# Where the butterflies of gate's and up's weights are written: a tile of their own, or the loaded tile's places

## The chip, the cores and the metric

The kernel runs on one core of a Trainium2 chip. The metric is the device time of one execution in microseconds, the median of several runs. The engines are called PE (TensorE, the matmuls), DVE (VectorE), ACT (ScalarE), POOL (GpSimd) and SP (SyncE, which here issues nearly all DMAs).

## The reference

All numbers are float32. x has 8 sequences of 512 tokens with 512 features.

```python
xn = _layernorm(x, axis=-1)
s = _L0_attn_ref(xn, ...)          # q, k, v; phi = elu + 1; kv_sum = cumsum(phi_k * v); (phi_q * kv_sum) @ Wo.T + bo
g = _silu(_L0_ffn_ref(xn, ...))
x = x + s * g
...
x = fwht(x * SU_ug) / SCALE        # _L0_ffn_ref, fwht: Walsh-Hadamard transform over the last dimension
x_up = x @ W_up.T * (Wscale_ug[:INTER] * SCALE)
x_gate = x @ W_gate.T * (Wscale_ug[INTER:] * SCALE)
x = jax.nn.silu(x_gate) * x_up
x = fwht(x * SU_dp) / SCALE
x = x @ W_down.T * (Wscale_dp * SCALE)
```

W_up and W_gate are 2048 x 512, W_down is 512 x 2048. The transform of 512 features is linear, so it can be applied to the weights instead of the tokens: the kernel does that once, on the chip ("folding").

## The kernel before, in words

**Products.** Every matrix product is made with seven products of half-size blocks in place of eight (a Strassen-like scheme). The seven places have names, P1, P2, P7, P3, P4, P5, P6, in this order of storage. A weight tile `w` is 128 x (2, 7, 128): j, one of two halves of the rows contracted; s, one of the seven places; 128 columns. Four places (P1, P2, P7, P4) are loaded, the others are sums that DVE makes in `encode_weights` (lines 312 to 315, four additions of 128x256). A `group` (line 449) multiplies one such tile with all tokens of two sequences; PE works in three PSUM banks (px, py, pz), ACT copies px out (L470), and DVE adds such a copy to py or pz (L476).

**Order of the work.** The 8 sequences are taken in pairs p = 0 to 3. Each pair: attention (k, v, q for two groups of heads), then four units u of the feed-forward part (gate, up, each in two tiles f = u and f = u + 4), each unit's hidden block `ho`, and after units 1 and 3 a product with the down weights (L536) into tiles `dn`, one of which is `d_0`, `d_1` for the two sequences; they are stored to DRAM by `put_by` (L752) as d_d. In pair 0 the weights are raw. For u = 0, 1, 2 they are loaded by `first_w`, into tiles from the pool `wpool` (4 buffers). For u = 3 `weights_ahead` (L1061) does it while unit 1's down product is on PE, into tiles of the pool `t8`. After folding, the tiles of f >= 4 are combined with those of f - 4 (`inner_w`, L397 to 422: additions of 128x896 at L412, stores at L404), and from then on all weights come from DRAM in their final form. So all 16 foldings (8 of gate, 8 of up) fall in pair 0.

**One folding** is `folded_w` (L926 to 962), as three steps that an agenda spreads over the program: the raw load (`raw_w`, four DMAs at L354, the weights of four 128x128 blocks per j), `butterflies` (L934: a Hadamard step over two index bits, four DVE operations of 128x512 at L937 to L940), `fold` (L943: the other seven bits, as two products with the constant matrix `had`, L946, each of four passes of 512 columns, since float32 is done in four passes; ACT scales the result back into `w` at L952, four copies of 128x256), and `encode` (L955).

**Pools.** `t8` has 6 buffers of 8 KB in each partition (one has 2 x 7 x 128 or 2 x 2 x 512 floats). It holds `r` of the butterflies (L935), the gates `g` and ups `u`, the down outputs `dn`, the tiles `wd` of the down weights, `w` of unit 3, and more. A new tile takes a place that an earlier one used, and its first writer waits until the last reader of the earlier one is done; a store to DRAM is such a reader. Which instructions stand where on each engine is set by the scheduler of the framework from priorities, data and buffers; where `later` and `pace` (L77, L80) are used, small pieces of work are put behind given instructions. SP issues its DMAs in one queue in order, so a DMA that waits holds back those behind it.

**The down weights** are folded as well, in four columns of blocks (`butterflies_down`, L979 and L984, `fold_down`, L998 and L1004), on a tile `rd` of its own; the tiles `wd` get their sums through `down_w` (the additions show as L93 and L99 because `pace` and `catch_up` call them). POOL encodes some `ho` and co (L304 to 307) and multiplies gate with up (L802).

Of the kernel before, what the change touches and what calls it, by code (L numbers as in the profile page):

```python
# [8 lines left out]
F32 = mybir.dt.float32  # L9
AF = mybir.ActivationFunctionType  # L10
ALU = mybir.AluOpType
# [10 lines left out]
def kernel(  # L22
# [27 lines left out]
    nc = tc.nc  # L50
    P = 128
# [16 lines left out]
    t8 = ctx.enter_context(tc.tile_pool(name="t8", bufs=6))  # L68
# [5 lines left out]
    @contextmanager  # L74
    def background(behind=150):

        at = tc.cur_priority  # L77
        tc.cur_priority = at + behind
        yield
        tc.cur_priority = at  # L80
# [23 lines left out]
    at = 0  # L104
# [12 lines left out]
    had = const.tile([P, P], F32, tag="had", name="had")  # L117
# [192 lines left out]
    def encode_weights(eng, w):  # L310
        w = w.rearrange("p j s e -> p s j e") if len(w.shape) == 4 else w
        eng.tensor_tensor(w[:, P5], w[:, P7], w[:, P4], ALU.add)
        eng.tensor_tensor(w[:, P6], w[:, P5], w[:, P1], ALU.subtract)
        eng.tensor_tensor(w[:, P3], w[:, P2], w[:, P6], ALU.subtract)
        eng.tensor_tensor(w[:, P7], w[:, P1], w[:, P7], ALU.subtract)
# [30 lines left out]
    def raw_w(name, src, n0, dn, step, c0, dc, w=None):  # L346

        w = new_w(name) if w is None else w
        for a in range(2):
            tiles = src[:, c0 + a * dc : c0 + a * dc + P].rearrange("(n p) e -> p n e", p=P)  # L350
            for b in range(2):
                n = n0 + b * dn
                place = (P1, P2, P7, P4)[2 * a + b]
                nc.sync.dma_start(w[:, :, place, :], tiles[:, n : n + step + 1 : step])  # L354
        return w
# [41 lines left out]
    def inner_w(m, u, w0, w1):  # L397

        if u not in inner:
            inner[u] = dram.tile([P, 7, 2, 7, P], F32, tag=f"d_gu_{u}", name=f"d_gu_{u}")  # L400
        d = inner[u][:, :, ("gate", "up").index(m)]

        def store(c, t):
            nc.sync.dma_start(d[:, :, c, :], t)  # L404

        store(P1, w0[:, 0])
        store(P2, w0[:, 1])
        store(P4, w1[:, 1])
        t = xin.tile([P, 3, 7, P], F32, tag="x", name=f"s_{m}_{u}")

        def made(c, i, a, b, op):
            nc.vector.tensor_tensor(t[:, i], a, b, op)  # L412
            store(c, t[:, i])

        later(1.0, made, P5, 0, w1[:, 0], w1[:, 1], ALU.add, soon=True)
        later(1.0, made, P6, 1, t[:, 0], w0[:, 0], ALU.subtract, soon=True)
        later(1.0, made, P3, 2, w0[:, 1], t[:, 1], ALU.subtract, soon=True)

        def last():
            later(1.0, made, P7, 0, w0[:, 0], w1[:, 0], ALU.subtract, soon=True)  # L420

        later(0.0, at, 8, last, soon=True)
# [503 lines left out]
    def folded_w(name, src, f, room=None):  # L926

        w = raw_w(f"{name}_{f}", src, 0, 2, 1, f * P, NG * P, room)
        places = (slice(P1, P7 + 1, 2), slice(P2, P4 + 1, 3))
        rs = []  # L930

        def butterflies():
            t = t8.tile([P, 2, 2, 2, 2, P], F32, tag="t", name=f"r_{name}_{f}")
            r2, r = t[:, 0], t[:, 1]  # L934
            rs.append(r)  # L935
            a, b = (w[:, :, place, :] for place in places)
            nc.vector.tensor_tensor(r2[:, 0], a, b, ALU.add)  # L937
            nc.vector.tensor_tensor(r2[:, 1], a, b, ALU.subtract)
            nc.vector.tensor_tensor(r[:, :, 0], r2[:, :, 0], r2[:, :, 1], ALU.add)
            nc.vector.tensor_tensor(r[:, :, 1], r2[:, :, 0], r2[:, :, 1], ALU.subtract)  # L940

        def fold():
            for b in range(2):  # L943
                p = ps.tile([P, 2, 2, P], F32, tag="t", name=f"pw_{name}_{f}_{b}")
                tc.keep_in_program_order(
                    nc.tensor.matmul(  # L946
                        p.rearrange("p j a e -> p (j a e)"), had,
                        rs[0][:, b].rearrange("p j a e -> p (j a e)"), start=True, stop=True,
                    )
                )  # L950
                for j in range(2):
                    nc.scalar.activation(  # L952
                        w[:, j, places[b], :], p[:, j], AF.Copy, scale=su_ug[:, 2 * b + j : 2 * b + j + 1]
                    )
        def encode():  # L955
            encode_weights(nc.vector, w)
            folded[name, f] = w
            if f >= NU:
                with background():
                    inner_w(name, f - NU, folded[name, f - NU], w)  # L960

        return w, [(5, butterflies), (7, fold), (9, encode)]

    folded = {}
# [75 lines left out]
    def first_w(m, g):  # L1040


        if m == "gate":
            return folded_w(m, wgate_t, g)
        if m == "up":
            return folded_w(m, wup_t, g)
        name, eng = f"{m}_{g}", nc.gpsimd if m == "o" else nc.vector
        if m == "o":
            t = new_w(name)
            w = by_factor(t)  # L1050
            rows_w(w, wo_t, g, 2)
        else:
            t = w = raw_w(name, sources[m], 0, 2, 1, g * P, 2 * P)

        def encode():
            encode_weights(eng, w)
            keep_w(name, t)

        return w, [(5, encode)]

    def weights_ahead(u):  # L1061

        def begin(m, src, f):
            t = t8.tile([P, 2, 7, P], F32, tag="t", name=f"w_{m}_{f}")
            _, steps = folded_w(m, src, f, t)
            place = 10
            for _, step in steps:
                at(place, step)
                place += 7

        at_ = 2
        for m, src in (("gate", wgate_t), ("up", wup_t)):
            for f in (u, u + NU):
                at(at_, lambda m=m, src=src, f=f: begin(m, src, f))
                at_ += 12
# [65 lines left out]
    for i in range(7):  # L1141
        dst = had if i % 2 == 0 else had2
        s = src.rearrange("p (a t h) -> p a t h", t=2, h=1 << i)
# [18 lines left out]
    rs = rd[:, : 3 * NF * P].rearrange("p (i c e) -> p i c e", i=3, e=P)  # L1162
# [141 lines left out]
```

## Time and profile before

| | us |
|---|---|
| runs | 1551.83, 1550.75, 1551.32 |
| median | 1551.32 |
| profiled execution, span (its own time, first to last instruction) | 1552.4 |
| PE busy | 1523.8 |
| DVE busy | 1002.4 |
| ACT busy | 418.9 |
| POOL busy | 436.7 |

By stretches of the span (busy us of each engine, granted PE clock as a share of full speed):

| stretch | PE | DVE | ACT | POOL | clock |
|---|---|---|---|---|---|
| 0 to 70 (no folding yet) | 61.31 | 61.93 | 31.31 | 7.83 | 1.00 |
| 70 to 345 (the 16 foldings) | 264.18 | 213.63 | 98.30 | 71.38 | 0.99 |
| 345 to 1552.4 | 1198.26 | 726.81 | 289.25 | 357.47 | 1.00 |

A row of a timeline has the start in us, the duration in us, the engine, the line of the kernel, the operation, out<-in by the program's names, partitions x elements, the count of instructions run together (x4), and in brackets the idle time of the engine before it with what ended it. SPq means the queue of SP, where only issuing is shown. "f32" is the type. A share of a stretch in which PE is busy is an average: what matters is which wait ends last ahead of PE.

### The profile page before, as it was taken

To read this page: it belongs to the slowest core of one execution; us is meant where nothing else is said; L and a number is where in the kernel's file an instruction comes from. 1 tells how busy PE (TensorE), PEld (TensorE's weight loads), DVE (VectorE), ACT (ScalarE), POOL (GpSimd) and SP (SyncE) were. 2 spreads that over 40 slices of the span, in tenths; PEclk is the share of its full clock that TensorE was granted. 3 is DMA by queue.
4 is the path that set the end of the run, shared out by engine and by line. 5 is a ranking of instruction groups with operands and counts; after the bars stand their busy time and mean duration, and the time that the engine had idled before them with its cause. 6 is when DMAs were issued, how large, how long until landed. Compare 5 with 4: busy or idle time off the path is not lost.

```text
span 1552.4 us, 15693 instructions
## 1 busy us (share of the span) xinstructions
PE 1523.8 (98%) x5924; PEld 1121.3 (72%) x5924; DVE 1002.4 (65%) x1423; ACT 418.9 (27%) x664; POOL 436.7 (28%) x236
## 2 busy tenths in 40 slices
PE   7989999999999999999999999999999999999998
PEld 3436446746874588888884488888886478888887
DVE  7989787378867665516767674715675575533673
ACT  4452341141125411112114431111213431111211
POOL 1232233004320261205511144302621126210631
PEclk9999999999999999999999999999999999999999
DMA  8345877687985244354576344335574233535462
GB/s 276 98 141 176 258 250 240 214 276 261 267 283 162 90 154 160 95 166 164 166 265 235 93 143 149 114 119 186 175 245 155 87 112 102 191 100 174 164 258 81
DMA packets 197692, 273.31 MB, mean 176 GB/s; under 512 B 56816, under 2 KB 155120, under 8 KB 193392
## 3 DMA queue, kind: packets, MB, share of 16 engines
q1 hardware_dynamic: 197472, 272.27, 54.0%
q8 instruction: 47, 0.77, 0.2%
q14 instruction: 29, 0.24, 0.0%
q10 hardware_dynamic: 144, 0.03, 0.0%
HBM read 196.25 MB, written 76.02 MB: 175 GB/s over the span
## 4 chain that ended last, share of the span: by engine, by line
PE 90%; DVE 6%; DMA 1%; ACT 1%; issue 1%; SPq 0%; POOL 0%; POOLq 0%; DVEq 0%; ACTq 0%
PE px_gu L638 20%; PE px_dn L536 13%; PE pz_gu L638 10%; PE pz_dn L536 6%; PE py_gu L638 5%; PE px_k L460 4%; PE py_dn L536 4%; PE px_o L536 3%; PE px_v L460 3%; PE px_q L460 3%; PE px_up L460 2%; PE pz_o L536 2%; PE pz_k L460 2%; PE pz_v L460 2%; PE pz_q L460 2%; PE px_gate L460 1%
## 5 line engine op out<-in xcount | busy, mean ns | idle before, releaser
L638 PE MATMUL px_gu<-xo,w_gu 128*128 128x256 f32 x1456 | 347.7, 380 | 1.4 <-DVE sb_gu L648 1.4
L638 PEld LDWEIGHTS px_gu<-xo,w_gu 128*128 128x128 f32 x1456 | 275.7, 190 | 45.9 <-issue 5.0
L536 PE MATMUL px_dn<-w_down,ho 128*128 128x256 f32 x1024 | 228.7, 379 | 0.0
L536 PEld LDWEIGHTS px_dn<-w_down,ho 128*128 128x128 f32 x1024 | 194.6, 190 | 28.6 <-issue 2.4
L638 PE MATMUL pz_gu<-xo,w_gu 128*128 128x256 f32 x728 | 187.7, 380 | 1.1 <-DVE u L476 1.1
L838 POOL TENSOR_TENSOR u<-u,v 128x1024 f32<-128x1024 f32 x26 | 61.0, 2367 | 365.9 <-DVE u L676 347.4
L638 PEld LDWEIGHTS pz_gu<-xo,w_gu 128*128 128x128 f32 x728 | 137.5, 190 | 22.3 <-DVE u L476 1.5
L536 PE MATMUL pz_dn<-w_down,ho 128*128 128x256 f32 x496 | 112.5, 379 | 1.7 <-DVE u L476 1.7
L536 PEld LDWEIGHTS pz_dn<-w_down,ho 128*128 128x128 f32 x496 | 93.7, 190 | 16.4 <-DVE u L476 2.1
L638 PE MATMUL py_gu<-xo,w_gu 128*128 128x256 f32 x364 | 93.4, 379 | 0.0
L304 POOL TENSOR_TENSOR co<-co 128x512 f32<-128x512 f32 x8 | 14.6, 1829 | 266.3 <-DVE co L737 266.3
L883 POOL TENSOR_TENSOR s<-s,d 128x512 f32<-128x512 f32 x30 | 40.0, 1333 | 165.4 <-ACT d L882 165.4
L638 PEld LDWEIGHTS py_gu<-xo,w_gu 128*128 128x128 f32 x364 | 69.2, 190 | 9.4
L842 POOL TENSOR_TENSOR v<-v,r 128x1024 f32<-128x1024 f32 x26 | 60.9, 2361 | 26.9 <-DVE r L676 26.9
L460 PE MATMUL px_k<-xo,w_k 128*128 128x512 f32 x128 | 61.8, 606 | 0.0
L460 PE MATMUL px_v<-xo,w_v 128*128 128x512 f32 x128 | 60.6, 594 | 0.0
L460 PE MATMUL px_q<-xo,w_q 128*128 128x512 f32 x128 | 60.3, 592 | 0.0
L828 ACT ACTIVATE a<-a,cols_sb 128x512 f32<-128x512 f32 x26 | 18.7, 721 | 149.5 <-DVE a L676 147.8
L882 ACT ACTIVATE d<-d 128x512 f32<-128x512 f32 x31 | 19.5, 630 | 144.4 <-DVE d L551 124.7
L536 PE MATMUL px_o<-w_o,co 128*128 128x256 f32 x256 | 58.2, 379 | 0.0
L828 ACT ACTIVATE u<-u,cols_sb 128x512 f32<-128x512 f32 x52 | 36.9, 720 | 78.2 <-DVE u L676 75.0
L536 PE MATMUL py_dn<-w_down,ho 128*128 128x256 f32 x256 | 57.9, 379 | 0.0
(269 smaller groups left out, 2417.4 us busy)
## 6 DMA issues: line engine op xcount, KB each, us to landing
w_gu<-d_gu SPq DMA_DIRECT2D x91, 896.0 KB, 4.5
w_down<-d_down SPq DMA_DIRECT2D x56, 512.0 KB, 3.8
d_s<-o SPq DMA_DIRECT2D x8, 1024.0 KB, 5.7
d_d<-dn SPq DMA_DIRECT2D x8, 1024.0 KB, 7.7
d<-d_d SPq DMA_DIRECT2D x8, 1024.0 KB, 6.3
s<-d_s SPq DMA_DIRECT2D x8, 1024.0 KB, 8.1
y<-in_x_dram SPq DMA_DIRECT2D x8, 1024.0 KB, 6.4
out_dram<-y SPq DMA_DIRECT2D x15, 512.0 KB, 3.2
```

The source lines that it names most:

```text
L304: eng.tensor_tensor(o[..., P5, :], o[..., P7, :], o[..., P1, :], ALU.subtract)
L460: nc.tensor.matmul(p.rearrange("p a t -> p (a t)") if len(r.shape) == 2 else p, ws[k][:, i, :], r, start=(first and k == 0), stop=(k == n ...
L536: nc.tensor.matmul(p[:, c], t[:, (2 * g + c) * P : (2 * g + c + 1) * P], ws[i](k), start=(first and k == 0 and c == cs[0]), stop=(k == n - ...
L638: nc.tensor.matmul(p[:, lane], w[:, lane, i, :], x[:, i, :], start=(first and lane == 0), stop=True, skip_group_check=True,)
L828: nc.scalar.activation(g[:, m], g[:, m], AF.Silu, scale=col("w_gate", u + m * NU + a * NG))
L838: nc.gpsimd.tensor_tensor(r[:, m], ru1[:, m], rv[:, m], ALU.add)
L842: nc.gpsimd.tensor_tensor(rv[:, m], rv[:, m], rr[:, m], ALU.add)
L882: nc.scalar.activation(d, d, AF.Silu)
L883: (nc.vector if final and (a, s) == (1, 0) else nc.gpsimd).tensor_tensor(r, r, d, ALU.mult)
```

## The change

The butterflies are written into the places of the loaded tile `w`, and tile `r` is no longer taken from `t8`. The tile has 14 places (j, s), counted j * 7 + s; four for each j hold raw blocks, P1 (0), P2 (1), P7 (2) and P4 (4), which are 0, 1, 2, 4, 7, 8, 9, 11. The first operation writes a - b to the places 3, 5, 10, 12 (`spots(3, 7, 2)`), which hold nothing yet; the second writes a + b over a; the third writes a difference to 4, 6, 11, 13 (`spots(4, 7, 2)`); the fourth writes a sum over 0, 2, 3, 5 (`spots(0, 3, 2)`). `spots(at, *dims)` is an access pattern written by hand: a first place and two steps between places, two of each. The two products of `fold` then read places 0, 2, 4, 6 and 3, 5, 11, 13, four pieces of 128 columns, instead of one piece of 512. The number, the kind and the size of all operations on DVE, PE and ACT stay the same, as do all DMAs. In the changed file lines behind L929 are 3 higher: the butterflies are at L940, L941, L943 and L944, the fold's product at L950, ACT's copy at L955.

```diff
         places = (slice(P1, P7 + 1, 2), slice(P2, P4 + 1, 3))
-        rs = []
+        flat_w = w.rearrange("p j s e -> p (j s) e")
+
+        def spots(at, *dims):
+            o = flat_w[:, at : at + 1, :]
+            return bass.AP(o.tensor, o.offset, [o.ap[0]] + [[step * P, 2] for step in dims] + [[1, P]])
+
+        rs = [spots(0, 4, 2), spots(3, 8, 2)]
 
         def butterflies():
-            t = t8.tile([P, 2, 2, 2, 2, P], F32, tag="t", name=f"r_{name}_{f}")
-            r2, r = t[:, 0], t[:, 1]
-            rs.append(r)
             a, b = (w[:, :, place, :] for place in places)
-            nc.vector.tensor_tensor(r2[:, 0], a, b, ALU.add)
-            nc.vector.tensor_tensor(r2[:, 1], a, b, ALU.subtract)
-            nc.vector.tensor_tensor(r[:, :, 0], r2[:, :, 0], r2[:, :, 1], ALU.add)
-            nc.vector.tensor_tensor(r[:, :, 1], r2[:, :, 0], r2[:, :, 1], ALU.subtract)
+            nc.vector.tensor_tensor(spots(3, 7, 2), a, b, ALU.subtract)
+            nc.vector.tensor_tensor(a, a, b, ALU.add)
+            a, b = spots(0, 3, 2), spots(7, 3, 2)
+            nc.vector.tensor_tensor(spots(4, 7, 2), a, b, ALU.subtract)
+            nc.vector.tensor_tensor(a, a, b, ALU.add)
 
         def fold():
             for b in range(2):
                 p = ps.tile([P, 2, 2, P], F32, tag="t", name=f"pw_{name}_{f}_{b}")
                 tc.keep_in_program_order(
                     nc.tensor.matmul(
-                        p.rearrange("p j a e -> p (j a e)"), had,
-                        rs[0][:, b].rearrange("p j a e -> p (j a e)"), start=True, stop=True,
+                        p, had, rs[b], start=True, stop=True,
                     )
                 )
```

## The prediction

> **What bounds the kernel now.** I read the chain that ended last first, then the idle times of TensorE (PE), then what stood ahead of the one that this change touches. The page's busy row and its row of the chain by engine:
>
> ```profile
> PE 1523.8 (98%) x5924; PEld 1121.3 (72%) x5924; DVE 1002.4 (65%) x1423; ACT 418.9 (27%) x664; POOL 436.7 (28%) x236
> PE 90%; DVE 6%; DMA 1%; ACT 1%; issue 1%; SPq 0%; POOL 0%; POOLq 0%; DVEq 0%; ACTq 0%
> ```
>
> PE works 1523.8 of 1552.4 us, so the end is set by PE. The change adds and removes no matmul; it can only make PE's gaps (28.6 us in all) smaller or larger, and change the clock after them. All 16 foldings run between 70 and 345 us. PE's timeline there has eleven gaps of 0.2 us or more: 68.51 (0.21), 77.73 (1.23), 106.60 (3.72), 113.56 (0.69), 138.62 (0.54), 207.49 (0.69), 256.27 (1.71), 304.93 (2.24), 365.22 (0.82), 370.03 (1.10), 382.04 (1.38). Only one of them waits for a butterfly. PE's timeline there (start, duration; idle before it in brackets):
>
> ```profile
> 299.72 2.97 PE L536 MATMUL pz_dn<-w_down,ho 128*128 128x256 f32 x13
> 304.93 2.45 PE L946 MATMUL pw_gate<-r_gate,had 128*128 128x512 f32 x4 [2.24 <-DVE r_gate L940]
> 307.17 3.13 PE L460 MATMUL px_gate<-xo,w_gate 128*128 128x512 f32 x4
> 310.13 1.88 PE L460 MATMUL py_gate<-xo,w_gate 128*128 128x512 f32 x4
> ```
>
> Four passes take 1.88 us at full clock, but 2.45 and 3.13 behind this gap: 0.57 and 1.25 us more. The granted clock of that fortieth of the span is 0.96, and 1.00 elsewhere. So the gap costs 2.24 + 0.57 + 1.25 = 4.06 us. Why was VectorE (DVE) late?
>
> ```profile
> 289.53 0.69 DVE L551 TENSOR_TENSOR dn<-sc_dn,pz_dn 128x512 f32<-128x512 f32 x1 [1.71 <-ACT sc_dn L545]
> 299.27 0.69 DVE L551 TENSOR_TENSOR dn<-sb_dn,pz_dn 128x512 f32<-128x512 f32 x1 [9.05 <-PE pz_dn L536]
> 301.68 0.69 DVE L937 TENSOR_TENSOR r_gate<-w_gate 128x512 f32<-128x512 f32 x1 [1.73 <-DMA d_d<-dn]
> 302.29 0.69 DVE L938 TENSOR_TENSOR r_gate<-w_gate 128x512 f32<-128x512 f32 x1
> 302.89 0.68 DVE L551 TENSOR_TENSOR dn<-sb_dn,pz_dn 128x512 f32<-128x512 f32 x1
> 303.49 0.69 DVE L939 TENSOR_TENSOR r_gate<-r_gate 128x512 f32<-128x512 f32 x1
> 304.10 0.69 DVE L940 TENSOR_TENSOR r_gate<-r_gate 128x512 f32<-128x512 f32 x1
> 307.41 0.69 DVE L937 TENSOR_TENSOR r_gate<-w_gate 128x512 f32<-128x512 f32 x1 [2.63 <-PE pw_gate L946]
> ```
>
> L937 waited for a store, dn to d_d, which has nothing to do with weights: tile r takes the t8 slot of an output block that must first be out. The weights had been asked for long before, the store only just (SyncE's queue):
>
> ```profile
> 280.28 1.97 SPq L354 DMA_DIRECT2D w_gate<-in_wgate_t_dram  x4
> ...
> 296.80 0.40 SPq L752 DMA_DIRECT2D d_d<-dn  x1
> ```
>
> Raw loads land 2.9 us (median) after their issue, so w_gate_2 was whole near 285, while DVE stood idle for 9.05 us.
>
> **The change part by part.** (Lines of the changed file are 3 higher behind L929; I use the old ones.)
>
> *The slot wait, removed.* The four butterflies (4 x 0.69, issued 0.60 apart, some 2.5 us) can run as soon as their weights are there. In the built order of the changed program those of w_gate_2 and w_gate_6 stand in DVE's idle stretch 284 to 299. The fold then finds its input ready when PE's L536 ends at 302.69. What is late next? The two PSUM tiles of pw_gate are free, and the fold waits for no ACT copy. I take the whole 4.06 us. Bounds: 0 (something else is as late) and 4.06. **-4.06.**
>
> *Butterflies, same number, same sizes.* 16 x 4 tensor_tensor of 128x512 before and after; only places differ. Rows with steps (L937, L938 read places with a step) and without (L939) both take 0.69, and in-place encodes (L315) take 0.42 like the others. No price.
>
> *The fold's moving operand with a step.* L946 reads one piece of 512; L460 reads two pieces of 256 with a gap between, and both take 0.59 a pass. Four pieces of 128 are shown nowhere. Bounds: 0, and 64 passes x 0.59 = 38 us if it doubled. Nearest row is L460, so 0.
>
> *Three waits of DVE on itself per folding for one.* In the built program each in-place butterfly after the first waits for the one before it. Price of one, from this row pair:
>
> ```profile
> 253.60 0.68 DVE L938 TENSOR_TENSOR r_gate<-w_gate 128x512 f32<-128x512 f32 x1
> 254.32 0.69 DVE L939 TENSOR_TENSOR r_gate<-r_gate 128x512 f32<-128x512 f32 x1
> 254.93 0.68 DVE L940 TENSOR_TENSOR r_gate<-r_gate 128x512 f32<-128x512 f32 x1
> 255.53 0.68 DVE L476 TENSOR_TENSOR u<-sb_up,pz_up 128x512 f32<-128x512 f32 x1
> 258.74 0.69 DVE L305 TENSOR_TENSOR ho<-ho 128x512 f32<-128x512 f32 x1 [2.52 <-POOL ho L802]
> ```
>
> L939 needs L938 and starts 0.72 behind it; independent ones start 0.60 apart: 0.12 each. Two more for 16 foldings: at most 32 x 0.12 = 3.8 us of DVE, where no other operation stands between. Most have one between, so 0 to 3.8, on the path only where DVE is what PE waits for. The Trainium skill ("VectorE: DVE Perf Modes", The DRAIN you can't avoid) says that semaphores between chained operations add nothing; by it this item is 0. The rows above show 0.12, and the rows decide.
>
> *Moves around it*, from comparing the two built orders on each engine. PE, ACT and POOL execute the same sets; the order differs only locally.
> - 60 to 107: DVE is busy without a break up to L476 g at 103.93 (four scans of L729 before it), the same operations stand ahead of it, so the 3.72 gap stays: 0 (bounds -0.3, +0.7, six butterflies' waits).
> - 138.62: L476 g stands one 0.60 issue earlier, but L944 (new line) ends just in time for the fold: -0.17 of 0.54 (bounds -0.54, +0.1).
> - 207.49 and 214: two butterflies of w_up_5 move ahead of L476 g; ACT's copies behind it come up to 1.3 us later and PE has 1.2 us of other matmuls: +0.1 (bounds -0.7, +0.7).
> - 256.27: PE waits for L476 u, now with two dependent waits more ahead: 0.24 less what other operations fill, +0.15 (bounds 0 and 2.1).
> - 260.7: two butterflies, one of w_gate_7 and one of w_up_3 (its loads now leave earlier), stand between L476 u and L305. L305 waits for POOL's L802 to 258.71, and the second butterfly is not done by then: L305 to L307 come 0.69 + 3 x 0.12 = 1.05 later, L307 is done near 261.1 instead of 260.03, and the pz_dn that needs it can start at 260.68: +0.45 (bounds 0 and 2.35, L802's length).
> - 305 to 385: DVE has two foldings less there (8 x 0.60 = 4.8 us), g of gate 2 now waits for a slot behind the store of dn (near 310; its bank is needed at 316), the 2.25 wait of L476 u at 339.78 goes. PE comes 4 us earlier and DVE's work some 4.8: 0 for the gaps 365, 370, 382, which sum to 3.3 (bounds -1.5, +2.8).
> - SyncE: the same DMAs; w_up_6's loads stand behind wd_0's, which wait for that store until 301.6: up to 0.6 late, with its fold ten us off: 0.
>
> **Sum:** -4.06 - 0.17 + 0.1 + 0.15 + 0.45 + 0 = -3.53 us. The profiled span is 1552.4, the runs' median 1551.32, so a run is 1.1 shorter than the span that I count in; the difference is carried over: 1551.32 - 3.53 = **1547.8**. A measurement of this kernel tells about 0.2%, 3.1 us: faster means below 1548.2.
>
> **Rivals.**
> A. *Given back at the next unit.* If PE arrives 4 us earlier while DVE's chain (L412 s tiles, L93, L300, L476) at 340 to 382 isn't earlier, the gaps there grow by up to 2.8. For: all three wait for DVE, and under POOL its L93 takes 1.48. Against: DVE loses 4.8 us of work there and 2.25 of slot wait. Time: 1547.8 + 2.8 = 1550.6, same.
> B. *Collision with POOL at 256 to 261, the slower side.* A DVE operation beside one of POOL's is stretched:
>
> ```profile
> 248.61 1.75 DVE L938 TENSOR_TENSOR r_gate<-w_gate 128x512 f32<-128x512 f32 x1
> ...
> 256.36 2.35 POOL L802 TENSOR_TENSOR ho<-g,u 128x1024 f32<-128x1024 f32 x1 [6.54 <-DVE u L476]
> ```
>
> (1.75 against 0.69.) If butterflies of w_up_3 stand ahead of L476 u under POOL, the gap at 256.27 grows by 2 x 1.06 = 2.1, the one at 260.7 becomes 2.35, and both bring the slow clock seen behind 304.93 (2 x 1.82 = 3.6): 8.1 in all against the 3.8 of the other terms (-4.06 - 0.17 + 0.1 + my 0.3): about 1551.3 - 4.1 + 8.1 = 1555.3. It decides once these two gaps grow by over 4.1 + 3.1 = 7.2 with the clock. For: L305 already waits for L802 there. Against: PE has other matmuls (px_dn, L946) to place, and only one of the two butterflies must precede L476.
> C. *The gap stays.* The butterflies are made early but the fold waits for something as late. For: PE's fold now also waits on the load queues. Against: those loads landed 17 us earlier. 1551.3, same.
>
> **Chances.** Forecast 0.62 (0.50 of it below 1548.2, 0.12 just above), A 0.17, B 0.16, C 0.05. Faster 0.50, same 0.12 + 0.17 + 0.05 = 0.34, slower 0.16. Low end: the sum with 365 to 382 at -1.5, 207 at -0.7 instead of +0.1, nothing at 260.7: 1547.8 - 2.75 = 1545.0. High end between A and B, 1553.5, which leaves out most of B. The forecast's own range is 1546 to 1549.
>
> **What would show it.** Right: no idle time ahead of the fold near 303, its four passes at 1.88, and the granted clock of that fortieth at 1.00; DVE's butterflies of gate 2 between 284 and 299; L946's passes at 0.59. Wrong: passes over 0.60 (the step costs), a gap over 2 us at 256 to 261 with a dip of the clock, gaps at 340 to 385 that sum to over 4 us, or a new wait ahead of the fold.

## The result, and the profile after

The changed kernel took 1554.28 us (median of 18 runs), the kernel before 1551.49 (18 runs, timed beside it): a ratio of 1.0016, interval 1.0009 to 1.0023. It is slower, by 0.16% where 0.23% less was forecast. In two comparisons made for the experiments, both on one chip (number 7; the chip of the first comparison is not on record), the ratio was 1.0001 (0.9992 to 1.0010) and 1.0001 (0.9991 to 1.0011), with the kernel before at 1555.25 and 1555.13. So the summary is: no gain, and a loss of 0.16% in the first comparison that the later two don't show. Ratios are over fast executions alone: one of after_g5 (4068.51 us) and the profiled one of first_g5 (6472.64 us, granted clock 0.236) are left out, so no profile of first_g5 is read. What has to be explained is where a gain that is plainly in the trace went.

In every run that gives both, the time is 1.8 us above the span (1554.91 against 1553.1 for the changed kernel's profiled run). The profiled execution of before, span 1552.4, therefore stands for a run of 1554.2, not 1551.3: 2.7 us above the median of 1551.49. Where that profile was taken is not on record; among the later runs of the kernel before, with medians from 1554.11 to 1555.25, such a run would be an ordinary one.

The busy row and the chain by engine of the changed kernel:

```profile
PE 1524.6 (98%) x5924; PEld 1121.6 (72%) x5924; DVE 1006.7 (65%) x1423; ACT 419.8 (27%) x664; POOL 432.6 (28%) x236
PE 88%; DVE 7%; DMA 3%; ACT 1%; issue 1%; SPq 0%; POOL 0%; POOLq 0%; DVEq 0%; ACTq 0%
```

PE's share of the chain fell by 2 points; DVE and DMA have them. PE's timeline of the changed kernel near 305:

```profile
299.31 7.07 PE L536 MATMUL pz_dn<-w_down,ho 128*128 128x256 f32 x32
306.21 1.88 PE L950 MATMUL pw_gate<-w_gate,had 128*128 128x512 f32 x4
307.93 1.88 PE L460 MATMUL px_gate<-xo,w_gate 128*128 128x512 f32 x4
309.65 1.88 PE L460 MATMUL py_gate<-xo,w_gate 128*128 128x512 f32 x4
```

No idle time in brackets, no slow passes: the fold of gate 2 waits for nothing, and its passes with a stepped operand take what they took before. The wait for the slot is gone. But the same timeline 50 us earlier, the kernel before first and then the changed one:

```profile
256.27 2.86 PE L536 MATMUL pz_dn<-w_down,ho 128*128 128x256 f32 x12 [1.71 <-DVE u L476]
```

```profile
253.41 1.89 PE L536 MATMUL px_dn<-w_down,ho 128*128 128x256 f32 x8
258.71 4.54 PE L536 MATMUL pz_dn<-w_down,ho 128*128 128x256 f32 x12 [3.41 <-DVE u L476]
263.09 1.88 PE L950 MATMUL pw_gate<-w_gate,had 128*128 128x512 f32 x4
```

The gap that was 1.71 us is 3.41, and the twelve passes behind it take 4.54 instead of 2.86. DVE of the changed kernel just before:

```profile
253.60 0.69 DVE L304 TENSOR_TENSOR ho<-ho 128x512 f32<-128x512 f32 x1
255.31 0.69 DVE L940 TENSOR_TENSOR w_gate<-w_gate 128x512 f32<-128x512 f32 x1 [1.01 <-DMA w_gate<-in_wgate_t_dram]
256.03 0.69 DVE L941 TENSOR_TENSOR w_gate<-w_gate 128x512 f32<-128x512 f32 x1
256.76 0.69 DVE L943 TENSOR_TENSOR w_gate<-w_gate 128x512 f32<-128x512 f32 x1
257.37 0.68 DVE L940 TENSOR_TENSOR w_up<-w_up 128x512 f32<-128x512 f32 x1
257.97 0.68 DVE L476 TENSOR_TENSOR u<-sb_up,pz_up 128x512 f32<-128x512 f32 x1
258.57 0.68 DVE L944 TENSOR_TENSOR w_gate<-w_gate 128x512 f32<-128x512 f32 x1
259.17 2.84 DVE L941 TENSOR_TENSOR w_up<-w_up 128x512 f32<-128x512 f32 x1
```

The sum u, for which PE waits, stands on DVE behind the butterflies of unit 3's second gate tile, and those now wait for their raw load. In the profile of before that load was there in time; the same butterfly had no wait:

```profile
253.00 0.68 DVE L937 TENSOR_TENSOR r_gate<-w_gate 128x512 f32<-128x512 f32 x1
```

**Where the time went, stage by stage.** Starts of the same matmuls in several profiles, each counted from the same early one (pz_k near 68); differences of two columns are stage lengths. The kernels named here are explained below.

| kernel | px_gate near 207 | first py_dn behind 262 | py_gate near 310 | pz_gu near 370 | last group, t_dn |
|---|---|---|---|---|---|
| before | 138.98 | 196.05 | 241.62 | 301.52 | 1476.21 |
| before, second profile | 138.94 | 198.88 | 242.72 | 302.77 | 1479.14 |
| changed | 138.82 | 199.78 | 241.18 | 300.61 | 1476.93 |
| changed, second profile | 138.69 | 200.90 | 242.30 | 301.73 | 1479.30 |
| changed, third profile | 138.86 | 199.79 | 241.19 | 300.61 | 1476.76 |
| fbu_g5 (best) | 138.81 | 196.42 | 237.82 | 297.24 | 1473.81 |

From 262 to 310 the changed kernel takes 41.40 us all three times, before 45.57 and 43.84: the gain of 2.4 to 4.2 is real. From 207 to 262 it takes 60.9 to 62.2, before 57.07 and 59.94: a loss of 1.0 to 5.1 us, by which executions are compared. From 310 to 370 it takes 59.4, before 59.9 and 60.1. From 370 to the end it takes 1176.3, 1177.6 and 1176.2, before 1174.7 and 1176.4: another 1.5 to 1.6 us is given back in the executions without slow passes near 380, and 1.2 between the two second profiles, which have such passes (clock 0.97 from 345 to 400).

### The profile page after: what moved, and what is told of

Same layout as the page of the kernel before. It is cut to its first block, busy times and chain, and to the rows that moved or that the text cites. A ratio compares the mean times of both kernels' runs of the same rounds, so it can differ in the third digit from the quotient of the medians.

```text
span 1553.1 us, 15703 instructions
## 1 busy us (share of the span) xinstructions
PE 1524.6 (98%) x5924; PEld 1121.6 (72%) x5924; DVE 1006.7 (65%) x1423; ACT 419.8 (27%) x664; POOL 432.6 (28%) x236
## 4 chain that ended last, share of the span: by engine, by line
PE 88%; DVE 7%; DMA 3%; ACT 1%; issue 1%; SPq 0%; POOL 0%; POOLq 0%; DVEq 0%; ACTq 0%
PE px_gu L638 19%; PE px_dn L536 13%; PE pz_gu L638 10%; PE pz_dn L536 7%; PE py_gu L638 5%; PE px_k L460 4%; PE py_dn L536 4%; PE px_o L536 4%; PE px_v L460 3%; PE px_q L460 3%; PE pz_o L536 2%; PE px_up L460 2%; PE pz_k L460 2%; PE pz_v L460 2%; PE pz_q L460 2%; PE px_gate L460 1%
## 5 line engine op out<-in xcount | busy, mean ns | idle before, releaser
L842 POOL TENSOR_TENSOR v<-v,r 128x1024 f32<-128x1024 f32 x26 | 60.9, 2366 | 26.3 <-DVE r L676 25.5
L460 PE MATMUL px_k<-xo,w_k 128*128 128x512 f32 x128 | 62.2, 609 | 0.0
```

The lines of the kernel that those rows point to most:

```text
L460: nc.tensor.matmul(p.rearrange("p a t -> p (a t)") if len(r.shape) == 2 else p, ws[k][:, i, :], r, start=(first and k == 0), stop=(k == n ...
L842: nc.gpsimd.tensor_tensor(rv[:, m], rv[:, m], rr[:, m], ALU.add)
```

## The experiments

All were timed in the same job as the kernel before. Ratios are to it.

**before_again**: no edit.

> The kernel before, unchanged, to see how far one profiled execution stands for all. The first profile of before has a span of 1552.4 us; the changed kernel's spans are 1.8 us below its times, so that profile would belong to a time of 1554.2, 2.7 us above the median of 1551.49. Theory 'the costed gap is not typical': the gap ahead of the fold of gate 2 is smaller than 2.24 us here or its slow clock (1.82 us) is missing, and the spans of the runs lie near 1549.7. Rival 'the profile was typical': the gap is 2.24 us with the slow passes again, and spans lie near 1552.4. Time by both 1551.5.

1.0002 (0.9994 to 1.0011). Its profile, PE:

```profile
256.94 4.54 PE L536 MATMUL pz_dn<-w_down,ho 128*128 128x256 f32 x12 [2.90 <-DVE u L476]
...
307.24 1.95 PE L946 MATMUL pw_gate<-r_gate,had 128*128 128x512 f32 x4 [2.20 <-DVE r_gate L940]
```

and DVE:

```profile
253.66 0.69 DVE L937 TENSOR_TENSOR r_gate<-w_gate 128x512 f32<-128x512 f32 x1 [1.05 <-DMA w_gate<-in_wgate_t_dram]
```

Both theories of the expectation are half right. The 2.20 us wait at 305 is there again, its slow passes are not (1.95 for four). And the gap at 256, which I had taken for fixed, is 2.90 with slow passes: the load was late here, with nothing changed. The time was not the expected 1551.5 but 1554.83: on this chip (number 14) the first profile's 1554.2 is a typical time.

**first_only** and **ahead_only**: the changed kernel with the old butterflies kept for part of the foldings.

```diff
         def butterflies():
+            if room is not None:      # ahead_only: if room is None
+                own_tile()            # the four old operations, into r from t8
+                return
```

> In place for the 12 foldings of units 0 to 2, a tile of their own from t8 for the four of unit 3. Theory 'place': the loss lies where unit 3's in-place butterflies came ahead of L476 u (gap 1.71 us before, 3.41 after, and 1.79 us of slow clock), the gain at gate 2's fold stays. Then the gap near 256 is 1.7 us again, the gap near 305 is gone, and the time is below before by 1 to 4 us: about 1549. Theory 'the writing in place costs' (self-waits, steps): 12 of 16 foldings carry three quarters of the loss of 2.8 us: 1553.6. Theory 'given back': the waits for x at 380 us (L140 ahead of L648) take back what is won ahead: 1551.5.

1.0003 (0.9994 to 1.0012). The gap at 305 is gone, the one near 256 is 4.06 us with 5.49 us for the twelve passes, although the butterflies there are the old ones in the old order. The theory "place", as put, fell: the loss isn't made by unit 3's in-place butterflies alone. Of the three theories' times only that of "given back" (1551.5, a ratio of 1.000) lies in the interval.

> The counterpart: in place for the four foldings of unit 3 alone, own tiles for units 0 to 2. Theory 'place': the gap near 256 is 3.4 us with slow passes behind it, the gap ahead of gate 2's fold near 305 is still there: 1554 to 1556. Theory 'the writing in place costs': a quarter of the loss, 1552.2. Theory 'given back': what is lost at 256 is in part taken up by the wait at 380: 1552 to 1553.

0.9996 (0.9987 to 1.0004): below all that the theories expected. Gap near 256: 1.80 us at full clock; at 305: 2.17 us with slow passes. PE comes to the gap 0.9 us later than in the first profile of before (counted from pz_k near 68), which shortens it. From 207 to 262 the stage takes 57.41 us, before 57.07 and 59.94. So in-place butterflies of unit 3, with one of an up tile ahead of u, don't make a large loss there by themselves.

**first_behind_u**, **before_behind_u**, **after_behind_u**: unit 3's butterflies, but for its first gate tile's, are issued behind the last sum of an up group, which is u. (first_only, before, and the changed kernel with this edit.)

```diff
+            def behind_output(step):
+                with tc.issue_after(last_out[0].ins):     # last_out: the newest L476
+                    step()
+
-            for _, step in steps:
-                at(place, step)
+            for i, (_, step) in enumerate(steps):
+                at(place, (lambda step=step: behind_output(step)) if i == 0 and (m, f) != ("gate", u) else step)
```

> As first_only, and the butterflies of unit 3's second gate tile and of its up tiles are issued behind the sum u that PE waits for near 256 (L476). Theory 'place': that gap, 1.71 us even in the kernel before, is gone, as is the one near 305: 1.7 us below first_only or more, about 1547. Theory 'given back': the gap at 382 (1.38 us before) grows by what was won, and the time stays at that of first_only, 1549 to 1551.

0.9982 (0.9973 to 0.9991), the first real gain. The gap near 256 is 0.45 us; a wait of 1.74 us comes up at the fold at 261, and 2.07 us at 379.

> The kernel before (tiles of their own), with unit 3's second gate butterflies and its up butterflies issued behind the sum u. Theory 'late load': the gap near 256 falls under 0.6 us, its slow passes go, the fold of that tile waits about 1.7 us at 261 (as in first_behind_u), the gap of 2.2 us at 305 stays: 0.9985 to 0.9995 of before. Rival 'the gain of first_behind_u came from the fold at 305': 1.000.

0.9991 (0.9982 to 1.0000), inside what was expected. 2.18 us of idle time and slow passes (2.64 for four) are still there at 305.

> The changed kernel, in place everywhere, with the same order forced. Theory 'late load': as first_behind_u, 0.998 of before, since the writing in place itself costs nothing on the path. Rival 'self-waits of DVE cost': the waits of the butterflies between u and the fold at 261 are exposed, 0.4 to 2 us above first_behind_u: 0.9985 to 0.9995.

0.9993 (0.9984 to 1.0002). The fold at 261 waits 2.34 us where it waited 1.74 in first_behind_u: the rival's direction, but the intervals of the two overlap, so a price for in-place butterflies isn't settled by this.

**after_again**: the changed kernel, no edit.

> The changed kernel, unchanged, beside the next three and the kernel before. In the last job the gap near 256 was 2.90 us with slow passes even in the kernel before, and 4.06 in a kernel with the same order of instructions there: the second gate tile's raw load lands late by an amount that differs from run to run (DVE waited 1.05 and 1.31 us for it; in the first profile of before it was there). Theory 'late load': the changed kernel adds to that gap the butterfly of unit 3's up tile (0.60) and two self-waits (0.24), no more: gap 3 to 4.5 us, slow passes behind it, none at 305; against before between 0.9995 and 1.0015. Theory 'in place costs everywhere': 1.0016 again, whatever the gap.

1.0001 (0.9992 to 1.0010); gap 3.64 us near 256, then 5.49 us for the twelve passes: as "late load" has it. The rival's 1.0016 lies outside the interval.

**x_behind** and **x_early**: two tries on the wait near 380, both on first_behind_u. The first issues the statistics of x behind the third sum of unit 3. The second gives this x a tile of t8, so that its load can leave earlier, and issues the statistics behind the first such sum.

```diff
+        t = t8.tile([P, NT, D], F32, tag="t", name=f"x_{b}") if b == 3 else None      # x_early alone
-        xt = load_x(b)
+        xt = load_x(b, t)
...
+        if b == 3:
+            at(30, behind_sum)     # layernorm and store under issue_after(last sum); 17 in x_early
+            return
```

> first_behind_u, and the layernorm statistics of x (L140), which stood ahead of the sums of unit 3 near 380 and made them wait for a load, are issued behind the third sum of that unit. Theory 'given back': the wait of 2.07 us at 379 and the two after it (0.26, 0.50) go, and the time falls by 2 to 3 us below first_behind_u: 0.9965 of before. Rival 'something else is as late there': no change, 0.998.

1.0046 (1.0034 to 1.0059). The wait at 379 went, but PE is busy for only 69.21 of the 80 us from 400 to 480. Most of that is one wait, 7.46 us at 443 (L547), for a load of w_down. On SP's queue the store of this x leaves at 404.83, in first_behind_u at 393.56, and the last loads of w_down at 436.53 instead of 431.14.

> first_behind_u with the last x of the first pair's loads in a tile of t8 instead of the one slot of the s tiles, so that its load needn't wait for the last s_up store; DVE's order near 380 is kept. Theory 'given back at the wait for x': the load leaves some 6 us earlier, the wait of about 2 us at 379 goes, and the time falls by 2 us below first_behind_u: 0.997 of before. Rival 'the sums of that unit are as late themselves': no change, 0.998.

1.0062 (1.0050 to 1.0074). PE of x_early:

```profile
372.42 3.68 PE L650 MATMUL px_gu<-xo,w_gu 128*128 128x256 f32 x8 [3.04 <-DMA w_gu<-d_gu]
...
459.38 9.78 PE L548 MATMUL pz_dn<-w_down,ho 128*128 128x256 f32 x32 [9.63 <-DMA w_down<-d_down]
```

Here, too, DVE no longer makes PE wait near 379; instead a load of w_gu does, and 87 us on a load of w_down. SP's queue is in another order: that load of w_down leaves at 453.34, behind two of y that hold the queue from 431.21 for 22.07 us; in first_behind_u the last one left at 431.14. That the wait for x takes time back is seen in the rows; that it can be had cheaply isn't.

**after_g5**, **first_g5**, **best**: two butterflies of unit 1's second up tile behind the sum g again (the changed kernel, first_only, and x_early with this edit).

```diff
+        def in_turn():
+            if (name, f) != ("up", 5):
+                butterflies()
+                return
+            with tc.issue_after(last_out[0].ins):
+                butterflies()
...
-        return w, [(5, butterflies), (7, fold), (9, encode)]
+        return w, [(5, in_turn), (7, fold), (9, encode)]
```

The reason is a chain that I found by comparing the two profiles backwards from the late load. DVE of before, and then of the changed kernel:

```profile
210.07 0.67 DVE L476 TENSOR_TENSOR g<-sc_gate,pz_gate 128x512 f32<-128x512 f32 x1
210.67 0.68 DVE L476 TENSOR_TENSOR g<-sa_gate,py_gate 128x512 f32<-128x512 f32 x1
...
227.84 1.09 DVE L412 TENSOR_TENSOR s_gate<-w_gate 128x896 f32<-128x896 f32 x1 [0.22 <-DMA d_x<-x]
```

```profile
209.87 0.67 DVE L476 TENSOR_TENSOR g<-sc_gate,pz_gate 128x512 f32<-128x512 f32 x1
210.47 0.68 DVE L940 TENSOR_TENSOR w_up<-w_up 128x512 f32<-128x512 f32 x1
211.19 0.69 DVE L941 TENSOR_TENSOR w_up<-w_up 128x512 f32<-128x512 f32 x1
211.80 0.68 DVE L476 TENSOR_TENSOR g<-sa_gate,py_gate 128x512 f32<-128x512 f32 x1
...
228.92 1.09 DVE L412 TENSOR_TENSOR s_gate<-w_gate 128x896 f32<-128x896 f32 x1 [0.99 <-DMA d_x<-x]
```

SP of before, and of the changed kernel:

```profile
223.63 0.37 SPq L190 DMA_DIRECT2D d_x<-x  x1
...
245.82 0.52 SPq L404 DMA_DIRECT2D d_gu<-s_up  x1
...
247.13 2.12 SPq L354 DMA_DIRECT2D w_gate<-in_wgate_t_dram  x4
```

```profile
224.72 0.37 SPq L190 DMA_DIRECT2D d_x<-x  x1
...
246.90 0.53 SPq L404 DMA_DIRECT2D d_gu<-s_up  x1
...
248.17 2.17 SPq L354 DMA_DIRECT2D w_gate<-in_wgate_t_dram  x4
```

g is 1.13 us later, the store of x 1.09 (the tile of x and the tiles s share one slot, so L412 waits for that store), L412 1.08, the last s_up store 1.08, the raw load 1.04. In these rows the whole delay is passed on, and the chain ends ahead of PE, 48 us from where it began.

> The changed kernel with one thing put back: the first two butterflies of unit 1's second up tile stand behind the sum g (L476) of its second gate tile again, as in the kernel before. In the changed kernel they stood ahead of it, 1.13 us, and from there everything on a chain was 1.1 us later: ACT's L784, the store of x that frees the slot of the s tiles, L412, its stores, the raw loads of unit 3's gate tiles (SP 244.34 against 243.27), the sum u. Theory 'the two butterflies ahead of g delay the loads': the loads leave 1.1 us earlier, the gap near 256 shrinks by about 1 us against the changed kernel, and the time falls by 1 us or, with fewer slow passes, 2: 0.999 of before. Rival 'the loss at 256 is made there, by the order of unit 3's butterflies': no change, 1.0005.

0.9992 (0.9981 to 1.0002): the ratio that the theory had, but not its gap, which is 3.21 us with slow passes. PE of after_g5:

```profile
257.41 5.49 PE L538 MATMUL pz_dn<-w_down,ho 128*128 128x256 f32 x12 [3.21 <-DVE u L477]
```

The load left earlier, but landed late: DVE's first use came 7.20 us after its issue, 5.87 in the first profile of before.

> In place for units 0 to 2, own tiles for unit 3, and the order at g put back: upstream of 256 as the kernel before in all that matters, and no wait for a slot at the fold of gate 2. Theory 'the two butterflies ahead of g delay the loads': the gap near 256 is that of the kernel before (1.7 to 2.9 us), the one at 305 is gone, some 1.5 us are given back at 382: 0.9985 of before. Rival: as first_only, 1.0003.

0.9994 (0.9986 to 1.0003): between the theory's 0.9985 and the rival's 1.0003, so it decides nothing.

> x_early and the order at g put back: all three fixes with in-place butterflies for units 0 to 2. If the three waits are separate, about 1 us below x_early: 0.9965 of before. If the wait at 99 us and the fold at 261 are what is left, the same as x_early.

1.0060 (1.0048 to 1.0072): the name is wrong, x_early's loss is all in it (9.77 us before L548 near 458).

**after_third**, **after_g5_again**, **before_delay**, **fbu_g5**: the deciding job, all on one chip. before_delay is the kernel before with

```diff
         def output(i, s, p):
+            for _ in range(2 if name == "gate_0_5" and i == 0 else 0):
+                nc.vector.tensor_tensor(dst[i], s, p.rearrange("p a t -> p (a t)"), ALU.add)
```

and fbu_g5 is first_behind_u with the edit of after_g5.

> The changed kernel once more, on one chip with the next three, since 1.0016 and 1.0001 differ by more than the term that is looked for. Theory 'the two butterflies ahead of g delay the loads': 1.000 to 1.0015 of before, a gap of over 3 us near 256 with slow passes.

1.0001 (0.9991 to 1.0011); gap 3.60 us, 4.33 for the twelve passes.

> The changed kernel with the two butterflies behind g again, on the same chip as the changed kernel itself. Theory: raw loads of unit 3's gate tiles leave 1.1 us earlier than in the changed kernel and the time is 0.001 of before lower. Rival 'not from there': same ratio as the changed kernel.

0.9994 (0.9985 to 1.0004), 0.0007 below after_third. PE and SP of after_g5_again:

```profile
256.27 2.86 PE L538 MATMUL pz_dn<-w_down,ho 128*128 128x256 f32 x12 [1.90 <-DVE u L477]
```

```profile
246.86 2.22 SPq L354 DMA_DIRECT2D w_gate<-in_wgate_t_dram  x4
```

The load was in time, the gap is back near before's 1.71; in after_g5, the same kernel, it was not. What both profiles show is when the load leaves. Counted from px_gate near 207 it leaves at 40.8 to 40.9 in the three profiles of the changed kernel, at 40.1 and 40.0 with the two butterflies behind g, at 39.6 and 39.7 in before: 0.8 of the 1.2 us come from them. By the timings alone the difference from the changed kernel is too small to be certain: twice lower (0.9992, 0.9994 against 1.0001, 1.0001), each time with intervals that overlap.

> The kernel before with the suspected cost put in by hand and doubled: the sum g of unit 1's second gate tile (L476) is computed three times in a row into the same place, the same result each time, so that its last copy comes some 2.4 us later (two repeats, and two butterflies that the scheduler puts between). Nothing is in place. Theory: raw loads of unit 3's gate tiles leave 1 to 2.4 us later, the gap near 256 grows by that, and the time rises by 1 to 3 us: 1.0005 to 1.002. Rival 'there is slack on that chain': 1.000, the gap near 256 as before.

1.0023 (1.0013 to 1.0033). PE and SP of before_delay:

```profile
258.65 4.54 PE L538 MATMUL pz_dn<-w_down,ho 128*128 128x256 f32 x12 [4.17 <-DVE u L478]
```

```profile
248.08 2.12 SPq L354 DMA_DIRECT2D w_gate<-in_wgate_t_dram  x4
```

Counted from the pz_k near 68, the last g comes 2.55 us later than in before (in the changed kernel 1.17), and the load leaves at 180.85 here, 179.5 to 179.7 in the changed kernel, 178.6 in before (both). So the chain passes on 2.2 of 2.55 us: it has next to no slack. The delayed sum alone, with no butterfly in place, makes the kernel before slower by 3.9 us in the median (1559.00 against 1555.13), a little more than expected. Not all of that need go by the chain: the edit also makes PE wait 0.50 us at 214, for a copy of ACT, where before doesn't wait.

> The version that should be best: first_behind_u (in place for units 0 to 2, unit 3's later butterflies behind u) with the two butterflies behind g. If the loads still matter once u no longer waits for them, the fold at 261 waits less (1.74 us before): 0.9975 of before. If not, 0.998 as first_behind_u.

0.9976 (0.9967 to 0.9985), 1550.87 us against 1555.13: the best version, 4.3 us below before. PE of fbu_g5:

```profile
253.26 2.86 PE L538 MATMUL pz_dn<-w_down,ho 128*128 128x256 f32 x12 [0.28 <-DVE u L477]
...
260.01 1.96 PE L972 MATMUL pw_gate<-r_gate,had 128*128 128x512 f32 x4 [1.74 <-DVE r_gate L966]
...
377.71 1.13 PE L640 MATMUL px_gu<-xo,w_gu 128*128 128x256 f32 x4 [2.30 <-DVE sb_gu L650]
```

Neither 256 (0.28 us) nor 305 holds PE up much any more; what is left of the old gaps is the fold at 261 and the wait near 380. The fold waits 1.74 us as in first_behind_u, not less, and the intervals of the two kernels overlap; that the load still matters there was not seen.

## Why the prediction was wrong, point by point

The sign was wrong, and the time lies 0.8 us beyond the range. By the stages of the table, first profile against first, the forecast was -0.2 up to 207, +0.7 up to 262 (0.1 + 0.15 + 0.45), -4.1 up to 310 and 0 behind; measured were -0.2, +3.9, -4.2, then -0.5 and +1.6: together +0.7 instead of -3.5.

- **The slot wait, -4.06: right mechanism, mis-sized.** The idle time went wherever unit 2's butterflies are in place, and never elsewhere. It is worth 2.2 us of waiting (2.44 for the stage). The 1.82 us of slow passes behind it came in some executions and not in others: before, ahead_only and before_behind_u had them (gaps 2.24, 2.17, 2.18), before_again and before_delay did not (2.20 both). I had read one execution's accident as a term.
- **"207.49 and 214: two butterflies of w_up_5 move ahead of L476 g ... +0.1": the step that failed.** At PE it is right (px_gate near 214 came 0.1 us later, counted from the one near 207). But I asked only what PE does next there. With ACT's work behind g, which I noted as "up to 1.3 us later", x's normalization came 1.1 us later, and that chain went on over a store, a shared slot, L412 and SP's queue to a load 36 us later. before_delay shows that a delay there reaches the load with no butterfly in place, and after_g5 and after_g5_again that the load leaves 0.8 us earlier without this one. How much of the changed kernel's time goes by it is not settled: the two ratios are too near.
- **"256.27 ... +0.15": measured +1.7 to +1.9 us of gap against the first profile, +0.5 to +0.7 against the second, and the slow passes.** Three things add up: the load leaves 1.1 us later; from issue of its first part to DVE's first use it takes 6.9 to 7.4 us where DVE waits for it (before_again, all three of the changed kernel, first_only, ahead_only, after_g5, before_delay) and 5.9 and 6.0 in two profiles in which DVE doesn't wait (before, after_g5_again); and one more butterfly stands ahead of u. I had one profile, in which the load happened to be in time, and treated its margin as given.
- **"260.7 ... +0.45": not seen.** pz_dn at 264.80 starts without idle time; all before it is late already. The collision that it and rival B rest on is there: L941 took 2.84 us beside POOL's L802 against 0.69. The Trainium skill ("SBUF — State Buffer", Who interferes with whom) says that a DVE instruction with two inputs from SBUF contends with a GpSimd instruction that reads SBUF; the row agrees.
- **"305 to 385: 0": two terms of opposite sign.** From 310 to 370 the changed kernel gains 0.5 to 0.6 us; behind 370 it gives 1.2 to 1.6 back. There statistics of x (L140) stand ahead of the sum that PE waits for (L648), and wait for the load of x; in before, and then in the changed kernel:

```profile
380.70 0.69 DVE L140 BATCH_NORM_STATS2 st<-x 128x6 f32<-128x512 f32 x1 [3.28 <-DMA x<-in_x_dram]
381.31 0.67 DVE L648 TENSOR_TENSOR sb_gu<-px_gu,a 128x512 f32<-128x512 f32 x1
```

```profile
379.95 1.29 DVE L140 BATCH_NORM_STATS2 st<-x 128x6 f32<-128x512 f32 x2 [3.48 <-DMA x<-in_x_dram]
381.15 0.67 DVE L648 TENSOR_TENSOR sb_gu<-px_gu,a 128x512 f32<-128x512 f32 x1
```

  PE comes there 0.9 us earlier and waits longer: 1.38 us before (1.87 in its second profile), 2.13 to 2.34 in the changed kernel. The load lets the statistics start 0.7 us earlier, but two of them stand ahead of the sum instead of one, 0.6 us more, in all three profiles of the changed kernel. Two short waits behind it (0.27 and 0.49 us, near 391 and 394) are new in the first and third profile. That was rival A, with another wait than the one I named.
- **"60 to 107 ... 0": right in sum.** The wait of 3.72 us near 106 became two in the changed kernel's first profile, 2.04 near 99 and 1.70 near 106; in its second profile 2.02 near 99 with slow passes.
- **Self-waits and steps: as costed.** A butterfly behind its predecessor starts 0.72 later (255.31 to 256.03) against 0.60, and the fold's passes are unchanged at 1.88 for four.
- **The base.** I took a run for 1.1 us shorter than the span; it is 1.8 longer. The profile of before, whose gaps I subtracted from, stands for a slower run than any but one of the 18 beside the changed kernel.

Of the rivals, B was right in place (256 to 261, a gap beyond 3 us with slow passes) and wrong in cause: the butterflies between the late load and u took 0.68 and 0.69 us, so POOL stretched none of them. Like for like (second profile of before against the third of the changed kernel), the stages up to 370 give -0.1 + 1.0 - 2.4 - 0.6, and the end + 1.2 to 1.6: -1.0 to -0.5 us, which a measurement can't tell from none, as in the two later comparisons. Why the first comparison showed +2.8 stays open: the kernel before was 2.6 to 3.8 us faster in it (1551.49) than in the later ones. Whether the load lands in time there as a rule was not tried.

## What to carry to other kernels

A wait that is removed lets the scheduler move instructions; follow each moved instruction through every engine and queue that waits behind it, until a wait with real slack ends the trail, and not only to the next matmul. A margin that one profile shows for a load is one draw: ask what the time is when it is used up. And what is won ahead of a wait for a DMA can be given back there, so look for the next such wait before counting a gain.

## What the runs showed of the hardware

Whether a short idle time of PE brings slow passes isn't decided by its length alone. Gaps of 1.71, 1.80 and 1.90 us near 256 brought none; all of 2.90 to 4.17 there did, for 1.5 to 2.6 us more in the twelve passes. But near 305 2.17 and 2.18 us did and 2.20 did not, twice; near 99 the changed kernel's gap of 2.04 did not (1.96 for four passes) and its 2.02 in the second profile did (2.97). Near 383 a gap of 1.87 did in before's second profile (1.33, 1.91 and 1.71 for three times four passes; in its first profile, behind 1.38 us, 1.13, 1.03 and 1.13). And one and the same gap, 3.72 us near 106, was followed by full clock in both profiles of before and in ahead_only (1.12, 1.12 and 1.13 for two passes), by slow passes in before_behind_u and before_delay (2.08 and 1.54). The Trainium skill ("TensorE: Matmul & The Clock Gate", Part 1, What's actually happening) gives an idle window of about 3.4 us for the drop of the clock; these rows show drops after 1.9 to 2.2 us, and after 3.72 only in two profiles of five, so it is no bound that can be planned with here. What decides it between 1.9 and 3.7 us was not found.
